# Third folding by DMA and a third layer every 16 steps in layer 0 of a four-layer attention kernel

## The chip, the cores and the metric

The kernel runs as one launch on one core of a Trainium2 chip. The metric is the device time of the launch in microseconds (us), the median of several runs. The engines are called here as in the profile: PE (TensorE, matmul; PEld its weight loads), DVE (VectorE), ACT (ScalarE), POOL (GpSimd), SP (SyncE, which here only issues transfers). A name with a q (POOLq, SPq) is the engine's instruction queue.

## The reference, cut to what matters

Four attention layers follow one another on x of 2 x 512 x 32 x 32 numbers in float32. The change is in layer 0, a deformable attention with 8 heads; layers 1 to 3 stay as they are. Each head has 64 sampled points (8 x 8) whose places come from a small convolution, and 1024 queries. The costly part is the position bias: for each of the 1024 queries and each of 64 points of every head a small network of two inputs, 128 and 128 hidden numbers and one output is run:

```python
pos = grid_q[:, :, None, :] - grid_kv[:, None, :, :]
bias = jnp.sign(pos) * jnp.log1p(jnp.abs(pos))
bias = jax.nn.relu(bias @ cpb_w1 + cpb_b1)      # 2 -> 128, "first"
bias = jax.nn.relu(bias @ cpb_w2 + cpb_b2)      # 128 -> 128, "second"
bias = (bias @ cpb_w3 + cpb_b3).reshape(b, GROUPS, H * W, Hd * Wd)   # 128 -> 1, "third"
sim = jnp.einsum('bhid,bhjd->bhij', qh, kh) + bias
attn = jax.nn.softmax(sim, axis=-1)
```

The output of the attention is projected and added to x, and an MLP with a hidden size of 2048 follows.

## The kernel before, in words

Layer 0 works on pairs of heads: NT = 8 pairs (2 images x 4 pairs), numbered t. A pair has 128 points; they are gone through four at a time, so a pair has NR = 32 steps and layer 0 has 256 steps, numbered i. The instruction order on every engine is that of the code (`in_order`), so a waiting instruction holds up everything behind it on its engine. A step does this:

- first (L526, DVE): for each of four points a 128 x 1024 tile, the hidden numbers of the first layer, is made from two small tables (`tab`, one for each axis). The point that is made is 7 ahead of the step (AHEAD = 7), and 11 tiles form the ring that it writes to: three of their own (`h1`) and eight in a weight buffer (`wa`). Hence the names wa and h in the profile's rows of L526.
- second (L543, PE; L552, ACT): in four parts, in the order 1, 0, 3, 2. In each part 32 of the 128 hidden rows of the second layer are made for all four points; the four 32-column matmuls stand side by side in one PSUM tile `z`, so its 128 rows are 4 points x 32 rows. ACT adds the bias and applies relu. `z` and all other short-lived PSUM tiles share three buffers of two banks (`zt`); a fourth pair of banks holds `sim`.
- joined (L557, DVE): the rows of the hidden layer were sorted at the start so that two parts can be added with the third layer's weights as +1 or -1 (`turn`). Part 0 is joined with part 1, and part 2 with part 3. A DMA with addition on POOL's queue (L832) then adds the two joins.
- folding by DMA (L825, L827, L829): in every second step the even rows and the odd rows of the sum are added (L825), and then the two steps' results are brought into one tile by a copy on SP's queue (L827) and another addition on POOL's (L829). What is left of two steps is one tile of 128 rows: 8 points x 16 rows.
- third (L571, PE): every 8 steps four such tiles are multiplied by `w3`, which holds signs, and are added up in `sim`.

A half step (the parts k = 1 and k = 3) ends with one turn of the side queue `behind`: a generator runs on to its next `yield`. The side queue holds, for pair t, `finish(t)` (softmax of the pair whose bias is complete, and after each image's fourth pair the projection with L629), `offsets(t + 2)` (places of the points, with the convolution's 36 products on ACT, six sums on DVE at L353, and at the end the store of the tables) and `samples(t + 1)` (keys and values at the points: weights `wy`, the product `pk`, then `kv`, `pkv`, `pvo`, and the small bias product `pb`, from which DVE makes `simbias`, L490). The `scores` matmul (L579) follows a pair's last third layer, and the side queue has to be empty by then.

Tables are loaded on SP's queue (L505) one chunk of 16 points ahead, and scaled on ACT (L513) in every fourth step. A chunk is 2 quarters of the pair's points x RCH = 8.

After the loop `finish_last` does the last pair's third layer, softmax and projection on their own, half by half. Then `layers` begins: it loads a bias table (`vb`), fills `ones` on POOL, and its first matmuls (`pmp`) wait for `xn`, which POOL makes (L1224).

Of the kernel before, what the change touches and what calls it, by code (L numbers as in the profile page):

```python
# [12 lines left out]
F32 = mybir.dt.float32  # L13
# [19 lines left out]
RCH = 8  # L33
# [47 lines left out]
def kernel(ctx: ExitStack, tc: tile.TileContext, a: dict, out: bass.AP):  # L81
# [56 lines left out]
    def layer0(l0, fold_d, t2_b, o2_b):  # L138
# [6 lines left out]
        h2j = l0.enter_context(tc.tile_pool(name="att_h2j", bufs=3))  # L145
# [79 lines left out]
        for w in (w3, w3_4):  # L225
            nc.gpsimd.memset(w, 0.0)
# [5 lines left out]
        def bias_weights():  # L232
# [3 lines left out]
            few = one.tile([P, 26], F32, name="few")  # L236
# [68 lines left out]
            nc.vector.tensor_scalar(w3[:, 24:32], w3[:, 24:32], w3sign[:, 1:2], None, ALU.mult)  # L305
            magnitude(b2h, w3_of)
# [14 lines left out]
        def offsets(t):  # L321
# [49 lines left out]
            if t:  # L371
                yield
            act = actbd[t % 2]
# [26 lines left out]
            yield  # L400
            sgn = two.tile([P, 2, 32], F32, name="sgn")
# [19 lines left out]
        def samples(t):  # L421
# [36 lines left out]
            yield  # L458

# [12 lines left out]
            yield  # L472
            pkv = zt([P, 2, P], "pkv")
# [9 lines left out]
            pvo = zt([P, C], "pvo")  # L483
            nc.tensor.matmul(pvo, values, ow, start=True, stop=True)
            vos[t] = vop.tile([P, C], F32, name="vo")
            nc.scalar.copy(vos[t], pvo)
            pb = zt([P, 1], "pb")
            nc.tensor.matmul(pb, kq, b1q[:, pr : pr + 1], start=True, stop=True)
# [4 lines left out]
        NCH = 2 * NR // RCH  # L493
        tabs_of = {}

        def load_tabs(c):

            t, rc = divmod(c, NCH)
            assert t in tables
            tabs_of[c] = []  # L500
            for ax in range(2):
                src = slog_d[t, ax].rearrange("(q r) i -> q r i", q=4)
                tab = two.tile([P, 2, RCH, 32], F32, name=f"tab{ax}")
                q, r = rc % 2 * 2, rc // 2 * RCH
                nc.sync.dma_start(out=tab, in_=src[q : q + 2, r : r + RCH, :].partition_broadcast(P))  # L505
                tabs_of[c].append(tab)
# [8 lines left out]
        def first(p):  # L515

            chunk, quad = divmod(p, 2 * RCH)
            quad, point = divmod(quad, RCH)
            if quad == 0 and point == 0:
                tabs_of.pop(chunk - 1, None)  # L520
                if chunk + 1 < NT * NCH:
                    load_tabs(chunk + 1)
            tx, ty = tabs_of[chunk]
            h1 = ring[p % len(ring)]

            nc.vector._custom_dve(  # L526
                TENSOR_ADD_SAT,
                out=h1.rearrange("p (y x) -> p y x", x=W),
                in0=tx[:, quad, point, :].unsqueeze(1).to_broadcast([P, H, W]),
                in1=ty[:, quad, point, :].unsqueeze(2).to_broadcast([P, H, W]),  # L530
                s0=float(np.finfo(np.float32).max),
                s1=0.0,
            )
            return h1

        def second(i, h1s, part):

            z = zt([P, HW], "z")
            lo = BLOCK[part]
            for half in range(2):  # L540
                n = slice(half * HALF, (half + 1) * HALF)
                for point in range(4):
                    nc.tensor.matmul(  # L543
                        z[point * 32 : point * 32 + 32, n],
                        cpb_w2[:, lo : lo + 32],
                        h1s[point][:, n],
                        start=True,
                        stop=True,
                    )
            ring = h2q if part % 2 else h2b if part else h2j if i % 2 else h2p  # L550
            h2 = ring.tile([P, HW], F32, name="h2", tag="h2")
            nc.scalar.activation(h2, z, AF.Relu, bias=b2h[:, part : part + 1])  # L552
            return h2
# [8 lines left out]
        def third(sim, r, h2s, fours=(), halves=range(2)):  # L562

            for half in halves:
                n = slice(half * HALF, (half + 1) * HALF)
                ways = [(quad, w3[:, 24 - r : 56 - r], h2) for quad, h2 in enumerate(h2s)]
                for k in range(2):
                    w = w3_4[:, 28 - r - 4 * k : 60 - r - 4 * k]
                    ways += [(quad, w, pair[k]) for quad, pair in enumerate(fours, len(h2s))]
                for k, (quad, w, h2) in enumerate(ways):  # L570
                    nc.tensor.matmul(  # L571
                        sim[quad * 32 : quad * 32 + 32, n], w, h2[:, n], start=(r == 0 and k < 4), stop=False
                    )
# [9 lines left out]
        def finish(t, sim):  # L583
# [4 lines left out]
            simb = two.tile([P, HW], F32, name="simb", tag="simb")  # L588
# [10 lines left out]
            at = two.tile([P, 8, P], F32, name="at", tag="simb")  # L599
# [10 lines left out]
            nc.vector.tensor_tensor(atv, atv, sm.unsqueeze(2).to_broadcast([P, 16, NJ]), ALU.mult)  # L610
            yield
# [29 lines left out]
        def finish_last(sim, eights, fours):  # L641
# [3 lines left out]
            table(AF.Exp)  # L645
            pps = [zt([P, HW], "pp")]
            project_out(pps[0], b, 0, range(2))
            simb = two.tile([P, HW], F32, name="simb", tag="simb")
# [4 lines left out]
            pt = zt([P, 8, P], "pt")  # L653
            ptv = pt.rearrange("p i (g j) -> p (i g) j", j=NJ)
            mx = two.tile([P, 16], F32, name="mx")
            at = two.tile([P, 8, P], F32, name="at", tag="simb")
            atv = at.rearrange("p i (g j) -> p (i g) j", j=NJ)
            sm = two.tile([P, 16], F32, name="sm")
            for half in range(2):
                g = slice(half * 8, half * 8 + 8)  # L660
                for i in range(half * 4, half * 4 + 4):
                    nc.tensor.transpose(pt[:, i, :], simb[:, i * P : (i + 1) * P], ident)
                nc.vector.tensor_reduce(mx[:, g], ptv[:, g], AX.X, ALU.max, negate=True)
            pps.append(zt([P, HW], "pp"))
            project_out(pps[0], b, 0, [2])
            project_out(pps[1], b, 1, range(2))
            for half, n in enumerate(halves):
                for g in range(half * 8, half * 8 + 8):
                    nc.scalar.activation(
                        atv[:, g, :], ptv[:, g, :], AF.Exp, bias=mx[:, g : g + 1], accum_out=sm[:, g : g + 1]  # L670
                    )
# [5 lines left out]
            for half, n in enumerate(halves):  # L677
                for i in range(half * 4, half * 4 + 4):
                    nc.tensor.transpose(pt[:, i, :], at[:, i, :], ident)
                nc.scalar.copy(aTs[b][:, pr, n], pt.rearrange("p i j -> p (i j)")[:, n])  # L680
                if half == 0:
                    project_out(pps[1], b, 1, [2])
            pps.append(ps_s.tile([P, HW], F32, name="pp", tag="sim"))
            for half, n in enumerate(halves):
                for m in range(3):
                    project_out(pps[m], b, m, range(NPAIR) if m == 2 else [pr], [half])
                    add_out(b, m, n, pps[m])
            pp = zt([P, HW], "pp")
            for half, n in enumerate(halves):
                project_out(pp, b, 3, range(NPAIR), [half])  # L690
                add_out(b, 3, n, pp)
# [121 lines left out]
        for i in range(steps):  # L813
            for k, part in enumerate((1, 0, 3, 2)):
# [5 lines left out]
                four = [h1s[4 * i + point] for point in range(4)]  # L820
                parts.setdefault(i, {})[part] = second(i, four, part)

                if i < steps - 2:
                    if i >= 2 and i % 2 == 0 and k == 0:
                        nc.gpsimd.dma_start(out=joins[i - 2][0:P:2], in_=joins[i - 2][1:P:2], accum_op=ALU.add)  # L825
                    if i >= 3 and i % 2 and k == 0:
                        nc.sync.dma_start(out=joins[i - 3][1:P:2], in_=joins[i - 2][0:P:2])  # L827
                    if i >= 3 and i % 2 and k == 3:
                        nc.gpsimd.dma_start(out=joins[i - 3][1:P:2], in_=joins.pop(i - 2)[1:P:2], accum_op=ALU.add)  # L829
                if k == 1 and i - 1 in parts:  # L830
                    other = joined(parts.pop(i - 1), 2)
                    nc.gpsimd.dma_start(out=joins[i - 1], in_=other, accum_op=ALU.add)  # L832
                if k % 2:
                    next(behind, None)
                if k == 3:
                    joins[i] = joined(parts[i], 0)
                due = i - 11
                if k == 1 and due >= 0 and due % 8 == 0:
# [3 lines left out]
                    third(sim, r, [joins.pop(due + j) for j in range(0, 8, 2)])  # L842
                    if r == NR - 8:
# [6 lines left out]
                        )  # L850
            for point in range(4):
# [201 lines left out]
    def layers(f, fold_d, t2_b, o2_b):  # L1053
# [9 lines left out]
        with nc.allow_non_contiguous_dma("1536 numbers"):  # L1063
            nc.sync.dma_start(out=vb, in_=a["vb"].rearrange("l (k p) -> p l k", p=P))
        gb3 = keep.tile([P, CC], F32, name="gb3")
        nc.vector.tensor_scalar(gb3, vb[:, 2, :], col("gamma3"), None, ALU.mult)
        ones = keep.tile([P, P], F32, name="ones1")
        nc.gpsimd.memset(ones, 1.0)
# [66 lines left out]
        with ExitStack() as mlp:  # L1135
# [108 lines left out]
            xn = normed(0)  # L1244
            hid = one.tile([P, HID // P, BLK], F32, name="hid")
# [6 lines left out]
            right1 = normed_rights(1)  # L1252
            for m in (2, 3, 0, 1):
# [972 lines left out]
```

## Time and profile before

| what | us |
|---|---|
| median of 3 runs | 3383.11 |
| lowest and highest run | 3380.47, 3383.16 |
| the profiled execution's own time | 3381.55 |
| its span, first to last instruction | 3379.8 |
| PE, DVE, ACT, POOL busy in the span | 3348.8, 2654.9, 1804.6, 464.7 |
| second layer's matmuls (two groups of L543), busy | 1779.1 and 986.3 |
| start of the main loop (first z matmul) | 57.66 |
| start of the MLP (first pmp matmul) | 2043.39 |

The granted clock of TensorE is 0.999 of full over the whole execution. In the page a group of instructions is one line: line of code, engine, operation, output <- inputs, sizes and count, then busy time and the mean of one, and the idle time of the engine ahead of it with what ended it. Matmuls of 32 columns run four side by side, so that the busy times of single ones overlap and their sum is more than the time that passed; a float32 matmul leaves two records. In a line of the timeline the numbers are start, duration, engine, line, operation, and in brackets the idle time before it with what it waited for.

### The profile page before, as it was taken

What the parts mean: (1) busy time and instruction counts of PE and PEld (TensorE: products, weight loads), DVE (VectorE), ACT (ScalarE), POOL (GpSimd) and SP (SyncE); (2) the same over time, 40 slices, a digit from 0 to 9 for tenths busy, and PEclk for the clock granted to TensorE, in tenths of its full rate; (3) what the DMA queues carried; (4) which work ended last, traced back from release to release, by engine and by line L of the source; (5) the groups of instructions that cost most, each with busy time, mean ns of one, the idle gap of its engine ahead of it and who ended that gap; (6) DMA issues with size and microseconds to landing.
All of it is one profiled execution on the core that took longest, in us unless ns stands there. A gap on an engine that the chain in (4) does not pass through costs nothing.

```text
span 3379.8 us, 61349 instructions
## 1 busy us (share of the span) xinstructions
PE 3348.8 (99%) x24861; PEld 1611.8 (48%) x24861; DVE 2654.9 (79%) x3458; ACT 1804.6 (53%) x2764; POOL 464.7 (14%) x563
## 2 busy tenths in 40 slices
PE   9999999999999999999999999999999999999999
PEld 4333333333333333333333337999953443687777
DVE  6999999999998899999999964464446566665656
ACT  4866867867866667867867651121226235122221
POOL 0222222222222122222222210000000000000000
PEclk9999999999999999999999999999999999999999
DMA  5676676676665476676676651000100000000111
GB/s 167 147 150 139 142 155 139 138 152 141 151 146 121 105 151 142 146 149 137 146 150 148 140 141 57 11 11 14 48 4 13 27 29 20 7 7 1 32 32 36
DMA packets 147284, 320.33 MB, mean 95 GB/s; under 512 B 31664, under 2 KB 77360, under 8 KB 146224
## 3 DMA queue, kind: packets, MB, share of 16 engines
q0 software_dynamic: 56880, 199.79, 31.1%
q1 hardware_dynamic: 88816, 111.81, 10.8%
q8 instruction: 198, 3.24, 0.4%
q10 hardware_dynamic: 1296, 4.72, 0.4%
q14 instruction: 94, 0.77, 0.1%
HBM read 71.46 MB, written 10.83 MB: 24 GB/s over the span
## 4 chain that ended last, share of the span: by engine, by line
PE 79%; DVE 15%; issue 4%; ACT 2%; DMA 0%; POOL 0%; DVEq 0%; SPq 0%; ACTq 0%; POOLq 0%
PE z L543 35%; DVE wa L526 6%; PE pw L1392 6%; PE pma L136 5%; PE pmb L136 4%; DVE h L557 4%; PE pmv L1392 4%; PE score L1571 3%; PE pv L1583 3%; PE pm L1392 3%; PE score L1392 3%; DVE h L526 2%; PE pmp L136 2%; PE pp L629 2%; PE pmt L1392 1%
## 5 line engine op out<-in xcount | busy, mean ns | idle before, releaser
L543 PE MATMUL z<-wa,cpb_w 128*32 128x512 f32 x11904 | 1779.1, 593 | 6.7 <-DVE simbias L490 3.4
L552 ACT ACTIVATE h<-z,b2h 128x1024 f32<-128x1024 f32 x1024 | 1134.9, 1114 | 529.1 <-PE z L543 505.7
L543 PE MATMUL z<-h,cpb_w 128*32 128x512 f32 x4480 | 986.3, 593 | 3.3 <-ACT h L552 2.2
L543 PEld LDWEIGHTS z<-wa,cpb_w 128*32 128x32 f32 x11904 | 493.0, 110 | 883.6 <-issue 804.2
L526 DVE CUSTOM_DVE_ANT_1 wa<-tab,tab 128x1024 f32<-128x1024 f32 x744 | 879.4, 1219 | 33.9 <-PE z L543 33.9
L557 DVE SCALAR_TENSOR_TENSOR h<-h,turn,h 128x1024 f32<-128x1024 f32 x512 | 654.7, 1279 | 8.8 <-ACT h L552 8.5
L543 PEld LDWEIGHTS z<-h,cpb_w 128*32 128x32 f32 x4480 | 256.3, 110 | 335.0 <-issue 292.0
L832 POOL DMA_DIRECT2D h<-h x255 | 227.2, 891 | 1062.4 <-DVE h L557 715.2
L526 DVE CUSTOM_DVE_ANT_1 h<-tab,tab 128x1024 f32<-128x1024 f32 x280 | 333.5, 1219 | 10.5 <-PE z L543 10.4
L1214 ACT COPY p<-pma 128x128 f32<-128x128 f32 x70 | 18.6, 266 | 305.5 <-PE pma L136 305.5
L1572 ACT ACTIVATE p<-score 128x512 f32<-128x512 f32 x256 | 130.0, 624 | 81.2 <-PE score L1571 80.4
L1206 DVE TENSOR_TENSOR upper<-pma,p 128x256 f32<-128x256 f32 x70 | 29.5, 422 | 163.4 <-ACT p L1214 163.3
L825 POOL DMA_DIRECT2D h<-h x126 | 109.6, 870 | 336.7 <-DMA h<-h 332.5
L829 POOL DMA_DIRECT2D h<-h x126 | 119.5, 948 | 133.0 <-DMA h<-h 126.7
L1604 DVE TENSOR_TENSOR acc<-acc,p 128x1024 f32<-128x1024 f32 x96 | 111.1, 1219 | 19.0 <-ACT p L1572 18.8
L1571 PE MATMUL score<-q,k 64*128 64x512 f32 x512 | 120.7, 604 | 1.1 <-DVE gm L1088 1.1
L1583 PE MATMUL pv<-p,vT 128*64 128x512 f32 x512 | 116.5, 598 | 0.0
L513 ACT ACTIVATE tab<-tab,pc 128x512 f32<-128x512 f32 x126 | 96.2, 763 | 0.0
L1392 PE MATMUL pmv<-wa,hc 128*128 128x256 f32 x384 | 89.7, 380 | 0.3 <-DVE u L1415 0.3
L347 ACT ACTIVATE products<-qpad,pc 128x64 f32<-128x64 f32 x252 | 85.5, 408 | 0.0
L1571 PEld LDWEIGHTS score<-q,k 64*128 64x128 f32 x512 | 47.3, 186 | 70.3 <-issue 54.9
L1392 PEld LDWEIGHTS pmv<-wa,hc 128*128 128x128 f32 x384 | 72.6, 190 | 14.2 <-issue 2.8
(451 smaller groups left out, 3708.5 us busy)
## 6 DMA issues: line engine op xcount, KB each, us to landing
h<-h POOLq DMA_DIRECT2D x255, 512.0 KB, 5.0
h<-h POOLq DMA_DIRECT2D x252, 256.0 KB, 4.8
tab<-slog_d SPq DMA_DIRECT2D x128, 256.0 KB, 4.5
h<-h SPq DMA_DIRECT2D x126, 256.0 KB, 2.3
r<-d SPq DMA_DIRECT2D x24, 256.0 KB, 3.5
xt<-in_xt SPq DMA_DIRECT2D x8, 512.0 KB, 7.8
wa<-in_mlp_w SPq DMA_DIRECT2D x4, 1024.0 KB, 7.8
wb<-in_mlp_w SPq DMA_DIRECT2D x16, 256.0 KB, 5.5
```

The costliest lines, as they stand in the source:

```text
L136: nc.tensor.matmul(pm, w, m, start=(k == 0), stop=(k == len(pairs) - 1))
L526: nc.vector._custom_dve(TENSOR_ADD_SAT, out=h1.rearrange("p (y x) -> p y x", x=W), in0=tx[:, quad, point, :].unsqueeze(1).to_broadcast([P, ...
L543: nc.tensor.matmul(z[point * 32 : point * 32 + 32, n], cpb_w2[:, lo : lo + 32], h1s[point][:, n], start=True, stop=True,)
L552: nc.scalar.activation(h2, z, AF.Relu, bias=b2h[:, part : part + 1])
L557: nc.vector.scalar_tensor_tensor(h2, h2, turn[:, part // 2 : part // 2 + 1], parts.pop(part + 1), ALU.mult, ALU.add)
L829: nc.gpsimd.dma_start(out=joins[i - 3][1:P:2], in_=joins.pop(i - 2)[1:P:2], accum_op=ALU.add)
L832: nc.gpsimd.dma_start(out=joins[i - 1], in_=other, accum_op=ALU.add)
L1392: nc.tensor.matmul(out, stationary(l, k), moving(r, k), start=start and k == 0, stop=k == nk - 1, skip_group_check=not start,)
L1571: nc.tensor.matmul(sc, ks[m][r, s * P : (s + 1) * P], qs[m][r, n], start=True, stop=True)
L1572: nc.scalar.activation(p[:, part], sc, AF.Exp, scale=64 ** -0.5)
L1583: nc.tensor.matmul(pv[half][part * 64 : part * 64 + 64], vt[s % 4][:, lo : lo + 64], lps[s, half][:, part, :], start=(s == 0), stop=(s == 7),)
L1604: nc.vector.tensor_add(acc[half], acc[half], ps[s, half])
```

## The change

It has six parts.

1. The folding goes one stage further. Of four steps (i, i+1, i+2, i+3) every one folds its odd rows onto its even ones, and a quarter of the rows of each is then added to another quarter: the first step in its own tile, the others by a copy on SP's queue into the first step's tile and an addition on POOL's queue. One tile of 16 points x 8 rows is left of four steps.
2. The third layer is done every 16 steps with a new sign table `w3_16`, at i = due + 20 ahead of part 0, where it had been at i = due + 11 behind it. The last 16 steps (from LAST on) keep the old way. With it the order of points, the table chunks (now 1 quarter x 16 points) and the rings of the h2 tiles change, and `scores` and the side queue begin one step later in the pair.
3. The bias product `pb` gets a column of `pvo`'s buffer and is issued ahead of `pvo`.
4. The side queue gets more turns: an additional `yield` in six places (only for later pairs in `offsets`).
5. The last softmax is done in two halves with a PSUM tile each, `pps[1]` takes `sim`'s banks, and all four output chunks go half by half.
6. In `layers`, `ones`, `vb` and `gb3` are made later. `simb` and `at` of `finish` share one buffer.

The diff, cut to its core:

```diff
-        h2j = l0.enter_context(tc.tile_pool(name="att_h2j", bufs=3))
+        h2j = l0.enter_context(tc.tile_pool(name="att_h2j", bufs=4))
...
+        w3_16 = one.tile([P, 48], F32, name="w3_16")
...
+            quarter = few[:, 26:28]
+            for k in range(2):
+                nc.vector.tensor_reduce(quarter[:, k : k + 1], ident[:, 2 + k : P : 4], AX.X, ALU.add)
+                nc.vector.scalar_tensor_tensor(eighth, quarter[:, k : k + 1], 8.0, eighth, ALU.mult, ALU.add)
+            nc.vector.tensor_scalar(w3_16[:, 16:32], row[:, 0:16], eighth, 0.0, ALU.add, ALU.is_equal)
+            nc.vector.tensor_scalar(w3_16[:, 16:32], w3_16[:, 16:32], w3sign[:, 1:2], None, ALU.mult)
...
# offsets: after table(AF.Gelu), and after table(AF.Ln)
             if t:
                 yield
+                yield
...
             yield
+            if t:
+                yield
...
# samples: after wy's product, after kv, and finish: after mx and after at's product
+            yield
...
-            pvo = zt([P, C], "pvo")
-            nc.tensor.matmul(pvo, values, ow, start=True, stop=True)
+            pvo = zt([P, HW], "pvo")
+            pb = pvo[:, C : C + 1]
+            nc.tensor.matmul(pb, kq, b1q[:, pr : pr + 1], start=True, stop=True)
+            nc.tensor.matmul(pvo[:, :C], values, ow, start=True, stop=True)
             vos[t] = vop.tile([P, C], F32, name="vo")
-            nc.scalar.copy(vos[t], pvo)
-            pb = zt([P, 1], "pb")
-            nc.tensor.matmul(pb, kq, b1q[:, pr : pr + 1], start=True, stop=True)
+            nc.scalar.copy(vos[t], pvo[:, :C])
...
-        NCH = 2 * NR // RCH
+        NCH = NR // 4
+        LAST = NT * NR - 16
...
-            ring = h2q if part % 2 else h2b if part else h2j if i % 2 else h2p
+            ring = h2q if part % 2 else h2b if part else h2j if i % (4 if i < LAST else 2) else h2p
...
-            pt = zt([P, 8, P], "pt")
+            pts = [zt([P, 4, P], "pt") for _ in range(2)]
...
-            at = two.tile([P, 8, P], F32, name="at", tag="simb")
+            at = h2q.tile([P, 8, P], F32, name="at", tag="h2")
...
-            pps.append(zt([P, HW], "pp"))
+            pps.append(ps_s.tile([P, HW], F32, name="pp", tag="sim"))
...
-                due = i - 11
-                if k == 1 and due >= 0 and due % 8 == 0:
+                due = i - 20
+                if k == 1 and 0 <= due < LAST and due % 16 == 0:
...
-                    third(sim, r, [joins.pop(due + j) for j in range(0, 8, 2)])
-                    if r == NR - 8:
+                    third(sim, r, [joins.pop(due + j) for j in range(0, 16, 4)], wide=True)
+                    if r:
...
+                four = [h1s[4 * i + point] for point in range(4)]
+                parts.setdefault(i, {})[part] = second(i, four, part)
...
+                if 0 <= i - 2 < LAST:
+                    j = (i - 2) % 4
+                    whole, own = joins[i - 2 - j], joins[i - 2]
+                    if k == 0:
+                        nc.gpsimd.dma_start(out=own[0:P:2], in_=own[1:P:2], accum_op=ALU.add)
+                    if k == 3 and j == 0:
+                        nc.gpsimd.dma_start(out=own[0:P:4], in_=own[2:P:4], accum_op=ALU.add)
+                    if k == 3 and j:
+                        nc.sync.dma_start(out=whole[j:P:4], in_=own[0:P:4])
                 if k == 1 and i - 1 in parts:
                     other = joined(parts.pop(i - 1), 2)
                     nc.gpsimd.dma_start(out=joins[i - 1], in_=other, accum_op=ALU.add)
+                j = (i - 3) % 4
+                if k == 1 and 0 <= i - 3 < LAST and j:
+                    nc.gpsimd.dma_start(
+                        out=joins[i - 3 - j][j:P:4], in_=joins.pop(i - 3)[2:P:4], accum_op=ALU.add
+                    )
...
+                due = i - 11
+                if k == 1 and due == LAST:
+                    third(sim, 16, [joins.pop(due + j) for j in range(0, 8, 2)])
...
# layers: moved behind xn = normed(0)
+            nc.gpsimd.memset(ones, 1.0)
+            with nc.allow_non_contiguous_dma("1536 numbers"):
+                nc.sync.dma_start(out=vb, in_=a["vb"].rearrange("l (k p) -> p l k", p=P))
```

## The prediction, made before the changed kernel was run

> **What bounds the kernel now.** First the page: shares of the engines and the busy tenths in 40 slices of 84.5 us.
>
> ```profile
> PE 3348.8 (99%) x24861; PEld 1611.8 (48%) x24861; DVE 2654.9 (79%) x3458; ACT 1804.6 (53%) x2764; POOL 464.7 (14%) x563
> ...
> PE   9999999999999999999999999999999999999999
> ...
> DVE  6999999999998899999999964464446566665656
> ```
>
> Layer 0 ends near 2043 us (slice 24). There two engines are full, and the share alone does not say which one sets the pace. So next the stretches: us, then PE, PEld, DVE, ACT, POOL busy.
>
> ```profile
> 200.00:300.00 100.00, 100.00 (x938) 30.29 (x932) 98.44 (x86) 66.51 (x63) 23.91 (x28) 1.00 0.72 151
> ```
>
> Then the chain of waits, in order of time, at the end of a head pair's turn (955 to 1045 us):
>
> ```profile
> 954.86 25.75 PE z L543 x240
> 980.61 1.72 PE sim L571 x16
> 982.33 54.93 PE z L543 x512
> 1037.26 1.72 PE sim L571 x16
> 1038.98 1.91 PE sim L579 x4
> ```
>
> Eight steps of the second layer take 54.93 us, 6.87 each, with nothing between them, and a third layer (L571, 16 records) takes 1.72 us of PE alone. Beside it VectorE, in its timeline at the same place:
>
> ```profile
> 1037.78 2.35 DVE L526 CUSTOM_DVE_ANT_1 wa<-tab,tab 128x1024 f32<-128x1024 f32 x2
> 1040.06 1.28 DVE L557 SCALAR_TENSOR_TENSOR h<-h,turn,h 128x1024 f32<-128x1024 f32 x1
> 1044.48 2.36 DVE L526 CUSTOM_DVE_ANT_1 wa<-tab,tab 128x1024 f32<-128x1024 f32 x2 [3.15 <-PE z L543]
> ```
>
> Two first layers start 2.28 us before their join, a join lasts 1.20 to the next start, so a step costs VectorE 2 x 3.47 = 6.93 us, 0.07 more than PE. VectorE catches up only while PE does something else, and here it stood 3.15 us. Last, who PE waits for in the first 2100 us:
>
> ```profile
> PE z L543 <- ACT h L552: 5.4, 11, 0.7
> PE z L543 <- DVE simbias L490: 4.5, 8, 0.6
> ```
>
> Ten microseconds in all: PE sets the end, VectorE is just behind.
>
> **A rule weighed.** The Trainium skill (Perfetto Trace Analysis, Identifying the Most-Contended Engine) says that matmul busy time is a bad measure and that weight-load busy time shows TensorE's headroom. By it PE, with 30% PEld above, is not the bound, VectorE with 98% is, and removing matmuls gives 0. The rows say otherwise: z matmuls start every 0.43 us in fours without a gap, and VectorE waits. I take the rows; the rule returns as a rival.
>
> **The change part by part.**
>
> *Third layers.* Before, 31 run inside the loop (520 records in all, less 24 of the last softmax, by 16). After, 15 wide ones and one of the old kind at the end: 15 fewer x 1.72 = 25.8 us, PE alone, with no other work beside them. The wide ones have the same shapes, so the same 1.72.
>
> *Does VectorE let PE have it?* From one scores (L579) to the next is 240.3 us. In 200 to 1000 us VectorE is idle 23.6 us of 800, so 7.1 per 240.3: it needs 233.2. PE after the change needs 240.3 - 2 x 1.72 = 236.9. On average it fits, by 3.7 us. Locally I follow the lag: start of first layer number 4i+7 (VectorE) after the start of step i (PE), counted from the two timelines (64 z records a step). Below 0.2 VectorE waits; PE waits when the lag plus 1.22 passes the step's time, about 5.6. Before, in the pair at 557 us, the lag at steps 10 to 20 of 32 is 0.2, 1.1, 0.3, 1.2, 2.2, 3.1, 4.1, 3.7, 4.6, 4.1, 2.4: six reductions L353 add 0.95 a step, the thirds at steps 11 and 19 take 1.72 off. Afterwards no third stands at 11. The pair at 1038 us shows that already, as four turns of output projection push its reductions past the third: 0.2, 1.1, 2.0, 3.0, 3.9, 4.9, 5.8, and the steps under it still take 6.87 (and 7.29 with the 0.43 of L379). The reserve was down to 0.26 us. So cost at the data: 0 to 0.5 us a pair; 0.3 taken into the sum below.
>
> *More turns.* A turn is half a step (3.43 us). Before 40 of 64 are used, after 46, so the side queue still empties in time. They separate VectorE's results from ACT or PE that use them. In the pair at 1038 us, pk (L461) came one turn after wy and its step took 9.96 instead of 6.87 + 2.2; elsewhere it took 9.45. With two turns a lag of 5 is covered. Gain: 0.4 x 6. Against it, ACT: samples move by about 2.5 steps onto step 21, where ACT also scales two tables (2 x 0.72). The same collision at 1200 us (near and wx L441 to L452 beside L513) stretched a step of 6.87 to 8.07. After, near stands half a step later, so I take 0.5 of that 1.2.
>
> *Bias product.* pb moves into pvo's buffer: the 0.54 us wait x 8 goes if the next z then takes another buffer, and stays if it takes this one, which is free only after the copy of pvo (0.59 us on ACT) and simbias. Bounds -4.5 and, with VectorE 1 us later there, +8.
>
> Together: waits on record 5.4 + 4.5 + 2.4 = 12.3, of which half goes: -6. New ones: ACT at step 21 0.5 x 6, lag 0.3 x 6, the wide third waiting for its data 0.2 x 6: +6.
>
> *Folds.* The landings and the issue on their queues:
>
> ```profile
> h<-h POOLq DMA_DIRECT2D x255, 512.0 KB, 5.0
> h<-h POOLq DMA_DIRECT2D x252, 256.0 KB, 4.8
> tab<-slog_d SPq DMA_DIRECT2D x128, 256.0 KB, 4.5
> h<-h SPq DMA_DIRECT2D x126, 256.0 KB, 2.3
> ```
>
> Per four steps POOL issues 4 x 512 + 4 x 256 KB before, and 4 x 128 KB more after; SP's copies go from 2 x 256 to 3 x 128 KB. POOL's queue moves 199.8 MB in 31.1% of the span, half the time within layer 0; a sixth more makes the DMA share 0.72 about 0.79, no bound. No trace row has the 128 KB size: by the page DMA: Bandwidth & Descriptors (Anatomy of one DMA) the estimate is 2.0 + 0.3 = 2.3 us, but by the same rule 256 KB would take 2.6, and it takes 4.8. I take 4.8 to 5.1. The last piece of a wide third is issued in step 18 after VectorE's join: lag 5.8 + 3.5, behind a 512 KB issue 0.9, landing 5.1: 15.3 us after that step's start. The third runs after 7.29 + 6.87 + 1.72 = 15.9. It fits by 0.6; with the longest landing of that line, 7.0, it is 1.3 late, 7 times, 9 us. The other wide thirds (step 4) have a lag under 2 and 4 us more. By 2.3 us all would fit.
>
> Behind POOL's waits stand qpad's memset and the next fold; behind SP's three copies the table load. That is asked for about three steps before it is scaled, 20 us, less 4.5 of landing and a wait of a step: 8 us left, else VectorE waits.
>
> *End of layer 0.* PE's waits 0.9 (L662 on mx), 0.5 (L679), 0.8 (L629 on x) go with two half tiles and the new order; ones' memset leaves POOL's way to xn, 0.5. Against: pps[0] is now the third buffer and waits for the last ACT h, which ends at 2004.30 while pp started at 2003.01: +1.3. Net -1.4. Further on nothing is touched; vb's load comes behind xn and is not awaited by PE.
>
> *Costed at nothing.* w3_16: six small VectorE instructions of 0.2 to 0.25 us, 1.3, before a wait of 2.21 us for th (L381); without it +1.3. simb and at in one buffer: at is written after pt has read simb anyway. Rings: h2j's four buffers are asked for again two steps after their last read. Uncovered, one late buffer costs a part, 1.7 us, a step.
>
> Sum against the profiled execution, 3381.55 (span 3379.8): -25.8 - 6 + 6 - 1.4 = **3354**. The three runs' median lies 1.6 above it, their spread is 2.7.
>
> **Rivals.**
> 1. *More goes* (0.22): the turns remove all 12.3 us and no new wait comes: 3381.6 - 25.8 - 12.3 - 1.4 = 3342. For it: the waits are all of the kind that turns cure. Against: the lag of 5.8.
> 2. *VectorE or ACT gives back about half* (0.20): the lag passes its limit in every pair; of 3.44 saved about 1.7 stays (25.8 / 2), 3367. For it: reserve 0.26, and 98% DVE; the rule above, taken whole, gives 3380. Against: 7.1 us idle a pair.
> 3. *POOL's loop sets the pace* (0.05, slower). Afterwards a fold stands in POOL's order in every step, not every other: a 512 KB issue must land before the fold behind it goes, and only then the next 512 KB issue. Now that is 5.0 + 0.84 = 5.8 us against 7.40 a step (236.9 / 32). It decides from 7.5, that is from a landing of 6.7; at 6.8 the 240 steps take 0.24 each, 57 us: 3411. For it: single landings up to 9.2 in the trace. Against: between 650 and 690 us they stay at 4.8 to 5.1 even with a fold beside them.
> 4. *The wide third doesn't save* (0.03): if it needed more passes, 1.72 x 2, the time stays at about 3380. Nothing in its shapes speaks for that.
>
> The sum itself has 0.50, with its own range 3348 to 3360 (bias product -4.5 to +8 about its share, the late fold up to +9 in part). Rivals 1 and 2 carry the same 3 us of looseness, so the range is 3339 to 3370. A measurement of this kernel tells about 0.2%, 6.8 us, from no change: faster than 3376.3 has 0.92 (the sum, rivals 1 and 2), within 0.03 (rival 4), slower 0.05 (rival 3).
>
> **What would show it.** L571 with 280 records (16 thirds in the loop x 16, and 24 of the end), two thirds a pair, and about 237 us from scores to scores. If simbias stays among PE's waits, the buffer step is wrong; waits of sim on DMA mean the late fold; steps 16 to 21 over 7.3 mean the lag or ACT. A first layer that never waits for PE means rival 2; POOL's fold always waiting, with landings above 6.5, rival 3. I am wrong if the pair still takes over 239 us.

## The result and the profile after

| | before | after |
|---|---|---|
| median of 6 runs each, us | 3381.39 (3380.30 to 3383.16) | 3355.55 (3352.63 to 3357.05) |
| ratio of the medians | | 0.9921, 95% interval 0.9908 to 0.9934 |
| profiled execution, own time, us | 3381.55 | 3353.20 |
| first z matmul to the last scores (L579, after L598), us | 1950.84 | 1925.62 |
| last scores to the first pmp matmul, us | 34.9 | 32.1 |
| first pmp matmul to the end of the span, us | 1336.4 | 1336.0 |

The change takes 25.8 us off the medians and 28.4 us between the two profiled executions: 25.2 in the main loop, 2.8 in the end of layer 0, 0.3 behind it. The forecast was 3354.

The page of after, as before from the shares down:

```profile
PE 3327.7 (99%) x24621; PEld 1611.4 (48%) x24621; DVE 2650.9 (79%) x3464; ACT 1802.6 (54%) x2764; POOL 674.5 (20%) x804
...
PE   9999999999999999999999999999999999999999
...
DVE  6999999999999799999999964455446465665556
```

PE has 240 records fewer, the 15 third layers of 16 records, and is as full as it was. POOL has 241 instructions more, 240 of them the new additions of 128 KB. The window of 200 to 300 us that was shown of before:

```profile
200.00:300.00 100.00, 100.00 (x940) 30.10 (x936) 100.00 (x88) 68.02 (x65) 36.35 (x42) 1.00 0.82 166
```

VectorE has no idle time left in this window (it was 98.44), and the DMA share is 0.82 instead of 0.72. The chain of waits at the same turn of a pair:

```profile
954.89 6.87 PE z L561 x64
961.76 0.42 PE pkv L485 x2
...
967.25 63.65 PE z L561 x592
1030.91 1.72 PE sim L590 x16
1032.62 1.91 PE sim L598 x4
```

A wide third takes the same 1.72 us for 16 steps that the old one took for 8. From scores to scores a pair takes 237.0 to 238.2 us instead of 240.3; the pair with the projection in it 265.6 instead of 270.9. Last, who PE waits for up to 2060 us:

```profile
PE z L561 <- ACT h L570: 5.3, 10, 0.5
...
PE z L561 <- DVE kvbd L479: 2.1, 2, 1.6
...
PE sim L590 <- DMA h<-h: 0.3, 1, 0.3
```

simbias and the idle before pk are gone; kvbd is new, in two steps only. The relu (L570) has 5.3 us where it had 5.4, at other places. VectorE's own waits tell why those places changed. Between 150 and 2000 us, first of before, then of after:

```profile
DVE wa L526 <- PE z L543: 33.9, 22, 3.1
...
DVE h L526 <- PE z L543: 8.3, 7, 3.1
```

```profile
DVE mx L616 <- PE pt L613: 26.8, 7, 4.5
...
DVE wa L544 <- PE z L561: 1.1, 1, 1.1
```

The first layer waited 42.2 us for PE and now waits 1.1: VectorE no longer catches up with PE inside a pair. It has not lost all its idle time: once a pair it now stands 3.8 us in the mean at the softmax's maximum (mx, 6.4 us in all before), until PE has done the transposes (pt) that come behind the wide third and the scores. As its order is fixed, it can't make first layers in that time.

### The profile page after: what moved, and what is told of

Same layout as the page of the kernel before. It is cut to its first block, busy times and chain, and to the rows that moved or that the text cites. A ratio compares the mean times of both kernels' runs of the same rounds, so it can differ in the third digit from the quotient of the medians.

```text
span 3351.4 us, 61296 instructions
## 1 busy us (share of the span) xinstructions
PE 3327.7 (99%) x24621; PEld 1611.4 (48%) x24621; DVE 2650.9 (79%) x3464; ACT 1802.6 (54%) x2764; POOL 674.5 (20%) x804
## 4 chain that ended last, share of the span: by engine, by line
PE 87%; DVE 7%; issue 2%; DMA 1%; ACT 1%; POOL 0%; SPq 0%; DVEq 0%; POOLq 0%; ACTq 0%
PE z L561 43%; PE pw L1431 6%; PE pma L135 5%; PE pmb L135 4%; PE pmv L1431 4%; PE score L1610 3%; PE pv L1622 3%; PE pm L1431 3%; PE score L1431 3%; DVE wa L544 3%; DVE h L575 2%; PE pp L650 2%; PE pmp L135 2%; PE ppr L1431 1%; PE pmt L1431 1%
## 5 line engine op out<-in xcount | busy, mean ns | idle before, releaser
L570 ACT ACTIVATE h<-z,b2h 128x1024 f32<-128x1024 f32 x1024 | 1134.3, 1113 | 505.6 <-PE z L561 466.5
L575 DVE SCALAR_TENSOR_TENSOR h<-h,turn,h 128x1024 f32<-128x1024 f32 x512 | 653.7, 1277 | 8.6 <-ACT h L570 8.6
L870 POOL DMA_DIRECT2D h<-h x240 | 203.7, 849 | 880.1 <-DMA h<-h 815.3
L877 POOL DMA_DIRECT2D h<-h x255 | 264.9, 1039 | 244.1 <-DVE h L575 152.1
L880 POOL DMA_DIRECT2D h<-h x180 | 224.9, 1249 | 4.3 <-issue 2.3
L532 ACT ACTIVATE tab<-tab,pc 128x512 f32<-128x512 f32 x126 | 95.7, 760 | 0.0
L1259 POOL TENSOR_SCALAR xn<-x,s,pc 128x256 f32<-128x256 f32 x32 | 19.1, 610 | 356.3 <-PE pma L135 241.9
```

Source lines behind the costliest of these rows:

```text
L575: nc.vector.scalar_tensor_tensor(h2, h2, turn[:, part // 2 : part // 2 + 1], parts.pop(part + 1), ALU.mult, ALU.add)
L870: nc.gpsimd.dma_start(out=own[0:P:2], in_=own[1:P:2], accum_op=ALU.add)
L880: nc.gpsimd.dma_start(out=joins[i - 3 - j][j:P:4], in_=joins.pop(i - 3)[2:P:4], accum_op=ALU.add)
```

## Where a pair's time goes, step by step

The table gives a step's time and VectorE's lag (as in the prediction), counted from the traces, for the pair whose scores before it stand at 558 us. "later" is the experiment e6_third_later below (569 us there); its side queue, and with it all but the tables, runs two steps later. A step without anything else takes 6.87.

| step of the pair | 16 | 17 | 18 | 19 | 20 | 21 | 22 | 23 | 24 | 25 | 26 |
|---|---|---|---|---|---|---|---|---|---|---|---|
| before, us | 7.29 | 6.89 | 7.64 | 8.58 | 6.87 | 9.46 | 7.65 | 8.81 | 6.87 | 6.87 | 6.87 |
| before, lag | 4.08 | 3.72 | 4.58 | 4.08 | 2.43 | 2.50 | 1.10 | 1.56 | 0.20 | 0.27 | 0.34 |
| after, us | 6.87 | 6.87 | 7.97 | 6.89 | 10.14 | 7.62 | 6.89 | 6.87 | 9.19 | 6.89 | 9.04 |
| after, lag | 4.73 | 5.68 | 6.63 | 5.60 | 6.56 | 3.49 | 2.88 | 2.92 | 4.12 | 1.87 | 2.52 |
| later, us | 6.87 | 6.87 | 6.87 | 6.87 | 7.29 | 6.89 | 9.34 | 7.01 | 6.95 | 6.87 | 9.18 |
| later, lag | 2.14 | 3.09 | 4.04 | 5.00 | 5.93 | 5.57 | 6.41 | 4.14 | 4.13 | 4.11 | 5.32 |

Three losses are new in after. Step 18 takes 7.97, of which 0.43 is the product with L379 (L386 now): 0.67 is lost, in five pairs. VectorE is 6.6 us behind, its join (L575) comes late, and ACT, which writes the odd parts into a ring of three tiles (h2q), waits for the join to free one. The timeline of ACT:

```profile
665.53 2.12 ACT L570 ACTIVATE h<-z,b2h 128x1024 f32<-128x1024 f32 x2 [1.36 <-DVE h L575]
```

Step 21 takes 7.62, 0.75 lost, in five pairs: near (L450, L451: with wx and wy it makes the weights of samples) and the scaled tables (L532) stand between ACT's relus, as the chain shows with z behind them:

```profile
687.44 1.11 ACT h L570
688.56 0.22 ACT near L450
...
689.50 0.19 ACT near L451
689.68 0.07 ACT tab L532
...
690.20 1.10 ACT h L570
...
691.35 20.81 PE z L561 x192
```

Step 20 should take 6.87 + 1.72 + 0.75 (gpb, L442) = 9.34. It takes 9.34 to 10.64, and step 4, which takes 11.77 in five pairs, takes 12.27 and 12.68 in two: together 4.3 us in which the wide third's last piece has not landed. PE's matmul hardly shows this wait (0.3 us above); the view of L880, the last folding, shows it on PE's weight loads:

```profile
  PEld sim L590: 3.7, 6
...
DMA to landing us min/median/max: 3.8/5.9/10.4
```

On the other side step 5, which waited for ACT with the softmax just behind it, went from 7.60 to 6.96, pk's wait is down by 0.27 and that for simbias by 0.54. So an ordinary pair loses 0.67 + 0.75 = 1.42 and wins 0.64 + 0.27 + 0.54 = 1.45, and 240.33 - 3.44 - 0.03 = 236.86. That is the pair without a late folding, 236.96 in after; what lies above it is the folding.

## The experiments

Each was timed, in four to thirteen runs, beside the kernel before on the same chip; the medians of before lay between 3380.9 and 3381.7. The ratios are to before.

**e4_thirds_out: half of the third layers taken out of the kernel before, nothing else.** Half of the position bias is then missing from the scores. The theory: fewer thirds alone give the 25.8. The rival: VectorE or ACT gives half back.

```diff
-                    third(sim, r, [joins.pop(due + j) for j in range(0, 8, 2)])
+                    eight = [joins.pop(due + j) for j in range(0, 8, 2)]
+                    if due % 16 == 0:
+                        third(sim, r, eight)
```

> The kernel before, with 15 of its 31 third layers (those at due = 8 mod 16) left out, so half of the position bias is missing from the scores; folding, turns and end as before. Theory PE (PE sets the end, 1.72 us of PE is 1.72 us of time): 15 x 1.72 = 25.8 us less, perhaps 3 to 6 of it given back where the lag then passes its limit: 3356 to 3361. Rival VectorE (its total work sets the pace of a pair): about half, 3368. Rival by weight-load share (PE has headroom): 3380.

Measured: 3365.53 us, ratio 0.9953 (0.9940 to 0.9967): -15.4 us. A pair goes from 240.3 to 238.6. The third at step 3 saves its whole 1.71 (10.63 to 8.92), the one at step 19 nothing: step 19 drops from 8.58 to 7.09, and step 21 rises from 9.46 to 10.95. PE's waits name it:

```profile
PE pk L136 <- ACT h L552: 10.7, 6, 2.1
```

The third at 19 had been the time in which VectorE's lag fell from 4.1 to 2.4. Without it the lag stays at 4.0, wy comes late, and pk, one turn behind wy, waits 1.7 us (2.1 once). (The row names ACT. The chain of waits has VectorE's wy from 691.62 to 692.84 us there, and pk starts at 692.9.) So the number of the second rival (3367) is about right for this kernel, by a handover of one turn and not by the general pace of VectorE, which is idle for 16.9 of the 800 us from 200 to 1000, 5 us a pair, elsewhere. Here a third saved its full length only where VectorE's results had not used it as slack.

**e1_turns_undone: after, without the six additional yields.** The theory: the turns keep the lag out of the handovers. The rival: the moved third does that already.

```diff
@@ in six places: offsets (2), samples (2), finish (2)
             yield
-            yield
```

> The changed kernel with the six additional turns taken out again. Theory turns (with fewer thirds VectorE's lag reaches 6 us, and what it hands to ACT or PE one turn, 3.4 us, later is then late): PE waits for pk behind wy as in the run with thirds left out, 1.5 us a pair, and ACT's relus wait behind the Gelu of acc, 1 us a pair, so 3365 to 3372. Rival (turns only move the side work): 3354 to 3357.

Measured: 3359.70 us (3357.59 to 3360.17), ratio 0.9936 (0.9922 to 0.9949): 4.1 us more than after. Both expectations missed, the theory by more than the rival. Step 17 takes 8.61 with a lag of 5.9, but the third at step 20 stands ahead of pk and brings the lag from 4.5 to 2.8. PE's waits:

```profile
PE z L556 <- ACT h L565: 9.9, 16, 1.2
PE pk L135 <- ACT h L565: 2.9, 2, 1.6
```

pk waits twice, not in every pair. Where the folding is not late a pair takes 237.51, against the 236.86 of after: the turns are worth 0.65 in it, and about 4 us in all by the medians. In e4 it took 238.6, so 1.1 us a pair come back without the turns. That the kept third stands just behind the reductions is one cause, as the lag shows; the move of pb may be another, as e4 still waits for simbias (0.5 a pair) and e1 doesn't. Neither was tried alone.

**e10_turns_alone: before, with the six yields.** The same question from the other side.

```diff
@@ in the same six places of the kernel before
             yield
+            yield
```

> The kernel before with the six additional turns alone. Theory (the turns are there for the lag that comes with fewer thirds; alone they push near and the tables onto one step and the reductions behind the third of step 11): no gain, 3380 to 3387. Rival (the waits on record in before, 2.4 for pk and some of ACT's 5.4, go): 3376 to 3378.

Measured: 3377.87 us, ratio 0.9990 (0.9982 to 0.9999): -3.8 us, with an interval from -6.1 to -0.3; the rival. Ordinary pairs are even 0.2 longer (240.54): step 21 has the ACT collision here too, 8.06. The pair with the projection goes from 270.85 to 268.54, the last from 218.11 to 216.88. So the turns are worth about 4 us with or without the rest of the change, but not in the same places: here where the side queue is fullest, at the end of an image, and in after in the ordinary pairs as well (e1).

**e2_pb_apart: after, with pb in a buffer of its own behind pvo.** The theory: the move is worth the wait for simbias, 4.5 us of before. The rival: with the turns there is nothing left to win.

```diff
-            pvo = zt([P, HW], "pvo")
-            pb = pvo[:, C : C + 1]
-            nc.tensor.matmul(pb, kq, b1q[:, pr : pr + 1], start=True, stop=True)
+            pvo = zt([P, C], "pvo")
...
+            pb = zt([P, 1], "pb")
+            nc.tensor.matmul(pb, kq, b1q[:, pr : pr + 1], start=True, stop=True)
```

> The changed kernel with the bias product in a buffer of its own again and behind the value product. Theory buffer (z waits for simbias because it gets pb's buffer): 8 waits of 0.5 us or, as VectorE is further behind, 1 us come back, 3360 to 3364. Rival (the turns removed the wait, the buffer nothing): 3355.

Measured: 3354.18 us (3353.55 to 3357.47), ratio 0.9922 (0.9909 to 0.9936), as after: the rival. The wait comes back, smaller:

```profile
PE z L561 <- DVE simbias L501: 2.1, 7, 0.4
```

The step of kv (26) takes 9.25 instead of 9.04, about 1 us over the five ordinary pairs, which the medians don't resolve.

**e3_end_alone: before, with the last softmax of after.** The edit is part 5 and 6 of the change as a whole (two PSUM tiles for pt, pps[1] in sim's banks, half by half, `ones`, `vb` and `gb3` later).

> The kernel before with the new end of layer 0 alone (last softmax by halves, and ones, vb and gb3 later, one buffer for simb and at). The two traces give 34.9 us from the last scores to the first MLP matmul before and 32.1 after. Theory: the whole 2.8 us is this part's own, 3378.6. Rival: only the 1.4 of the prediction's sum, the rest came from the loop's handing over, 3380. Rival: nothing, 3381.4.

Measured: 3379.06 us, ratio 0.9994 (0.9985 to 1.0002): -1.9 by the medians, which the interval does not tell from nothing. Its trace gives the theory's 2.8: the stretch from the last scores to pmp takes 32.1 us, the same as in after, against 34.9, and the pairs are unchanged at 240.3. The timeline of PE there:

```profile
2003.46 3.70 PE L629 MATMUL pp<-aT,vo 128*128 128x512 f32 x8
...
2041.07 4.19 PE L136 MATMUL pmp<-xn,wa 128*128 128x256 f32 x14 [0.89 <-POOL xn L1221]
```

pp starts right behind the last z: the wait for the last relu in the third buffer, which I had put at 1.3, does not come.

**e5_folds_out: after, with the second folding stage left out.** Three quarters of what a wide third adds up are then missing; PE, ACT and VectorE do the same work. The theory: a late folding costs several us. The rival: it costs what the trace's PE wait says, 0.3.

```diff
-                    if k == 3 and j == 0:
-                        nc.gpsimd.dma_start(out=own[0:P:4], in_=own[2:P:4], accum_op=ALU.add)
-                    if k == 3 and j:
-                        nc.sync.dma_start(out=whole[j:P:4], in_=own[0:P:4])
...
-                    nc.gpsimd.dma_start(
-                        out=joins[i - 3 - j][j:P:4], in_=joins.pop(i - 3)[2:P:4], accum_op=ALU.add
-                    )
+                    joins.pop(i - 3)
```

> The changed kernel with the second folding stage left out (the 128 KB additions and SP's copies), so three quarters of a wide third layer's inputs are missing from its sums; PE, ACT and VectorE do the same work. Theory late fold (in step 20 the wide third waits for the last 128 KB addition, 0.75 to 2.05 us a pair in the trace of after): 6 to 8 us less, 3348 to 3350, and step 20 takes 8.6. Rival lag (the step is long because VectorE is behind, the data would be there): no change, 3355. Rival DMA (the extra transfers slow others down as well): over 10 us less.

Measured: 3350.09 us, ratio 0.9909 (0.9894 to 0.9924): 5.5 us under after. All ordinary pairs take 236.85 to 236.89, step 20 always 9.34, step 4 always 11.77; steps 18 and 21 keep their 8.00 and 7.62. So the second stage costs about 5 us, and the other two losses have nothing to do with it. My figure of 8.6 for step 20 had forgotten gpb.

**e6_third_later: after, with the wide third two steps later.** This takes the lateness away and leaves every transfer in.

```diff
-                due = i - 20
+                due = i - (22 if i < LAST else 20)
```

> The changed kernel with the wide third layer two steps later (due = i - 22, the last pair's second wide one unchanged). The data are then there 14 us earlier than needed. Theory late fold: as without the fold, 6 to 8 us less, about 3348. Rival lag: the stall only moves, because VectorE's lag has no relief until step 22 and PE then waits for first-layer data in steps 19 to 21; 3355 to 3360.

Measured: 3350.98 us (3349.43 to 3351.61), ratio 0.9911 (0.9897 to 0.9924): 4.6 us under after, and no run of it is as long as the shortest of after. The pairs take 236.70 to 236.72, the step with the third 9.34 every time. And a second thing is seen in the table: with the other third of the pair now at step 6 and the softmax's steps behind it, the lag is down to 0.3 before the reductions instead of 1.0; step 20 with its product takes 7.29 at a lag of 5.9, so the ring costs nothing there; and the collision of step 21, now in step 23, has shrunk to 0.14 (7.01). These 1.28 us are not won, though: the pair is only 0.16 shorter than in e5. Step 9 now takes 7.59, as the softmax's exponentials and the tables meet on ACT there, and step 27 takes 7.28, where VectorE's kvbd is late. In the trace the main loop is 2.6 us shorter than in after (3.7 than in after_again, below); of the rest, some stands ahead of the loop, which starts between 55.8 and 59.5 us in the traces whatever the edit.

**e8_h2q4: after, with a fourth tile in h2q's ring.** The theory: step 18's 0.67 goes. The rival: the next stall takes it.

```diff
-        h2q = l0.enter_context(tc.tile_pool(name="att_h2q", bufs=3))
+        h2q = l0.enter_context(tc.tile_pool(name="att_h2q", bufs=4))
...
-        ones = one.tile([P, P], F32, name="ones")
...
-            shift = one.tile([P, P], F32, name="shift")
+            shift = one.tile([P, P], F32, name="shift", tag="shift")
...
-            kq = one.tile([P, P], F32, name="kq")
+            kq = one.tile([P, P], F32, name="kq", tag="shift")
```

> The changed kernel with four buffers instead of three for the odd parts of the second layer (room from one shared small tile and from ones replaced by a broadcast column). Theory relu buffer (step 18 takes 7.97 instead of 7.30 because ACT's relu waits for the join of a part three steps of a part earlier, 1.4 us in the waits of after): 0.67 x 5 and a little of the first pair, 3351 to 3352, step 18 at 7.3. Rival lag at the data (PE lacks first layers): no change, 3355, step 18 at 7.9.

Measured: 3355.49 us (3353.90 to 3356.39), ratio 0.9923 (0.9910 to 0.9937), as after. Step 18 goes from 7.97 to 7.39, so the ring was what ACT waited for. But PE then meets the third sooner while VectorE is no faster: the lag rises to 7.0, step 20 takes 10.52 instead of 10.14 (10.35 to 11.43 over the pairs), and step 4 up to 13.24. The late folding takes back all of it.

**e9_later_h2q4: both together.** The theory: with the third later, the fourth tile is worth its 0.6 a pair. The rival: with the lag at 5.9 there is nothing to win.

> The changed kernel with the wide third two steps later and four buffers for the odd parts, the two edits together. Theory (what four buffers save in step 18 was taken by the late fold in step 20, so it counts once the fold is early): 1 to 3 us below the later third alone, 3348 to 3350. Rival (with the third later the lag before the reductions is already lower and no relu waits for a buffer): as the later third alone, 3350 to 3352.

Measured: 3350.34 us (3350.13 to 3353.49), ratio 0.9912 (0.9898 to 0.9925), pairs 236.72: the rival. Of what was tried, one changed line, the third two steps later, is all that is worth adding to after.

**e7_samples_first: after, with samples ahead of offsets in the side queue.** The theory: with samples' PE work early in the pair and the six reductions late, the lag meets neither. The pair at the end of the first image keeps the old order, and samples has its two additional turns only there.

```diff
-        behind = chain(small_steps, offsets(1), samples(0))
+        behind = chain(small_steps, samples(0), offsets(1))
...
-                            offsets(t + 2) if t + 2 < NT else iter(()),
-                            samples(t + 1) if t + 1 < NT else iter(()),
+                            *(
+                                [offsets(t + 2), samples(t + 1)]
+                                if t == NPAIR - 1
+                                else [
+                                    samples(t + 1) if t + 1 < NT else iter(()),
+                                    offsets(t + 2) if t + 2 < NT else iter(()),
+                                ]
+                            ),
```

> The changed kernel with samples(t + 1) ahead of offsets(t + 2) in the side queue (but for the pair that ends an image), and without the two additional turns in samples: PE's extra products come first, the six reductions later, from step 18 on, with the wide third of step 20 among them. Theory lag: the lag stays below 5.5, so 0.67 in step 18, 0.75 in step 21 (ACT's near and tables together) and the late fold, 4 in all, go: 10 to 11 us less, about 3345. Rival: the collisions move to other steps, 3352 or more.

Measured: 3369.09 us, ratio 0.9967 (0.9954 to 0.9979): 13.5 us more than after; the theory fell, and the collisions moved, as the rival had it. Steps 18 to 21 are clean indeed (6.87, 6.87, 8.58, 6.87). But the lag that the reductions leave now stays, at 4.8 to 5.5, up to the next pair's step 4, where after has 2.5, and there the third's data are late. Step 4 takes up to 17.2 where 11.77 is its own work, with a landing on the chain of waits, and PE's waits have both handovers:

```profile
790.61 7.58 DMA h<-h
...
798.24 2.97 PE sim L592 x10
```

```profile
PE pk L135 <- ACT h L572: 9.4, 6, 1.6
PE sim L592 <- DMA h<-h: 8.9, 5, 2.7
```

This shows the chain from the other end: with the slack used up by VectorE's lag, the third waits for its data. How long, the lag alone doesn't say: at the same lag of 5.5 the step is between 0.7 and 5.4 us too long, by the landings.

**after_again: after once more,** beside e9 and e10, for its scatter.

> The changed kernel itself on the same chip as the two others, for comparison: 3355, the lag and the late fold as in its first trace.

Measured: 3356.16 us (3353.62 to 3357.22), ratio 0.9925 (0.9911 to 0.9938). One ordinary pair takes 239.51 here, the others 236.86 to 237.60. The pairs scatter where the folding is late and in no kernel where it is not.

## Why the prediction was right

- **The sum** held: 3354 against 3355.55. So did the sign and the range. The terms below say how much of it was understood.
- **Third layers, -25.8.** Shown as records (280) and as two thirds a pair, and their 1.72 us unchanged. But e4 gives only 15.4 for them alone. The prediction asked whether VectorE lets PE have the time, answered it on average (3.7 us to spare a pair), and looked for the local limit at the data. The local limit of e4 is a handover, wy to pk. In after it is gone: the turns account for about 4 us (e1, e10), and the rest came back without them (e1), by the place of the kept third or the move of pb.
- **The lag.** Its course was right: it was put at 5.8 from the pair at 1038 us and reaches 5.7 at step 17, 6.6 at 18. The limit that I gave, data late at 5.6, was the wrong one. ACT's ring comes first, at 0.67 in five pairs, 3.4 us in all where I had taken 1.8. PE's own rows name the first layer in no run; its weight loads wait for it 0.3 us at most in after, 0.5 in e8 and 0.9 in e7. So the limit is there, but later than 5.6: in e8 the lag of 6.7 with the 1.22 makes 7.9, and the step takes 7.39.
- **Waits that go, -6.** Mis-sized: simbias 4.5 and most of pk's 2.4 and of the relu's 5.4 (at step 5) go, about 11 of the 12.3, nearly as rival 1 had it. The runs show the turns as the cause for about 4 us (e1, e10). The buffer of pb is worth about 1 us by the steps, and nothing that the medians resolve (e2).
- **New waits, +6.** Mis-sized the same way: ACT at step 21 3.75 (0.75 in five pairs; I had 3.0), the ring 3.4, the late folding 4.3 to 5.5 (I had 1.2). Together 11 to 13. The two errors, of about 6 us each, have opposite signs and cancel; this part of the forecast was good by luck.
- **The late folding.** Its place, its trigger (the lag in step 18) and the bounds of 0 to 9 us were right; the weight of 0.2 a pair was too low. The sum of its step, done again with what the five ordinary pairs show: the last piece is issued 11.0 us after the start of step 18 (I had 10.2, as the lag is 6.6 and not 5.8), lands 5.4 to 6.8 later (5.1), so at 16.4 to 17.8 (15.3), and the third could run at 16.6 (15.9, without the ring's 0.67). The slack of 0.6 is gone in four of the five. At step 4, which I had called safe, the lag is 2.5 and the piece is late in two of seven pairs, where it is issued about 2 us later than in the others, behind a fold that had waited on POOL for a landing.
- **Landing of the 128 KB pieces.** Taken at 4.8 to 5.1, measured 5.9 on L880 (the median of 180) and 6.5 on the fifteen that a wide third waits for. The estimate of 2.3 by the Trainium skill (DMA: Bandwidth & Descriptors, Anatomy of one DMA) would have excluded the late folding altogether; it is well under half of what was measured.
- **End of layer 0, -1.4.** Measured -2.8: the term of +1.3 for the third buffer did not come.
- **Rivals.** The second named the right danger and the wrong lever. The third, POOL's loop: the 512 KB landing is 5.5, and by 7.40 a step it decides at 6.6 (the 6.7 was a slip); POOL waits 815 us in all for landings ahead of L870 and doesn't set the pace. The fourth did not happen. The rule of the Trainium skill (Perfetto Trace Analysis, Identifying the Most-Contended Engine), taken by weight loads alone as the prediction did, would have given no gain; the page names MFU, the share of the peak arithmetic, beside them, which was not worked out here. PEld is still at 30.10 in the window above, beside a PE that is the bound and gave 25 us.

What stays open: whether the last 128 KB piece would land sooner elsewhere in POOL's queue (the trace speaks for it, below; no run moved it alone), how the 1.1 us a pair that come back without the turns divide between the kept third's place and pb, and what the collision on ACT (step 21) costs, which no run took away by itself.

## What to carry to other kernels

Where two engines run at 98% and more, count how far the one is behind the other in program order, step by step; the averages say only whether it can catch up at all. Time taken off the engine that sets the end is also slack taken from the other: look up which handovers lived on it, and move them apart. What is left of the removed work may stand where the lag is highest; e4 and e1 speak for that, but it was not tried alone. And a stall that is removed ahead of a fixed meeting point (here the third layer and its transfers) is handed on to it; move the meeting point first.

## What the hardware showed that I had not expected

The landing of an addition by DMA follows what stands ahead of it more than its size. The rows of after, with the two rows of 256 and 512 KB that stood at 4.8 and 5.0 before:

```profile
h<-h POOLq DMA_DIRECT2D x255, 512.0 KB, 5.5
h<-h POOLq DMA_DIRECT2D x252, 256.0 KB, 3.5
...
h<-h POOLq DMA_DIRECT2D x240, 128.0 KB, 5.5
h<-h SPq DMA_DIRECT2D x180, 128.0 KB, 3.6
```

A quarter of the size takes as long as the whole, and longer than the half. The row of 128 KB mixes two lines of the same size and form. L880, whose landing of 3.8/5.9/10.4 stood above, is issued 0.54 us (median) behind a 512 KB addition. L872, which adds the same quarter of the rows in the first step's own tile, is issued 4.2 us behind one:

```profile
DMA to landing us min/median/max: 2.8/3.5/6.6
```

So 2.4 us of L880's landing are not its size. Issue by issue the trace ties it to what lies ahead of it in POOL's queue: not one of the 180 pieces lands before the 512 KB addition that was issued ahead of it; in the median it lands 0.65 us behind that. The pieces that a wide third waits for are the last of four steps; the 512 KB additions ahead of the last ones take 6.5 us in the median, and so do the pieces. For the third at 675 us the two issues are these, and they land after 6.2 and 6.3 us:

```profile
669.21 1.03 POOL L877 DMA_DIRECT2D h<-h  x1
669.75 1.34 POOL L880 DMA_DIRECT2D h<-h  x1
```

The kernel before shows the same in its folds of 256 KB: L829 lands after 5.7 us where it was issued less than 1.2 us behind a 512 KB addition (56 times), after 4.7 at 1.2 to 3 us (53) and after 4.0 at more (17). A common cause, other transfers that slow both, isn't excluded: no run moved the piece to try. The copies on SP's queue went from 2.3 for 256 KB to 3.6 for 128 KB, with the DMA share up from 0.72 to 0.82 beside them; why is open too.

POOL itself pays nothing for issuing two additions at once: an issue takes 0.85 us for L870, which stands alone, and L877 and L880 together take 1.74 (median) from the first's start to the second's end.
